# Eight transformer layers on one core: from layer after layer to one order for the whole program

## The chip, the cores and the metric

The kernel runs on one core of a Trainium2 chip. The metric is the device time of one launch in microseconds; the kernel before was run three times, and one more execution was profiled.

## The reference

A sequence model of four blocks, each an attention-like layer and a feed-forward layer with a layer norm in front and a residual around it: eight layers on x of 8 batch elements x 512 tokens x 128 channels, all float32.

```python
x = x + _L0_attn_ref(_layernorm(x), ...)   # 16 heads of 8; scores set to 0 where the key's 32-block is later than the query's
x = x + _L0_ffn_ref(_layernorm(x), ...)    # gated SiLU of width 352, inputs and weights rounded to FP4 in blocks of 16
x = x + _L1_attn_ref(_layernorm(x), ...)   # causal, with ALiBi; q, k, v weights plus low-rank terms
x = x + _L1_ffn_ref(_layernorm(x), ...)    # ternary weights: 128 -> 512 (gated) -> 512 -> 512 -> 128, two GELUs
x = x + _L2_attn_ref(_layernorm(x), ...)   # full attention, no output projection
x = x + _L2_ffn_ref(_layernorm(x), ...)    # channel mix with the previous token
x = x + _L3_attn_ref(_layernorm(x), ...)   # convolution of 4, scan with decay 0.95, gate, its own layer norm
x = x + _L3_ffn_ref(_layernorm(x), ...)    # 2 branches x 8 experts of rank 64, running sums, a softmax router
```

In the expert layer `Q = x W_Q^T` and `K = x W_K^T`, the second branch uses `Q W_inv^T` and `K W_inv^T`, each expert multiplies a projection of Q with the running sum of a projection of K, and the sum over experts goes through `W_O`. All of these maps are linear up to that product, and a running sum along the tokens commutes with a map of the channels.

## The kernel before

All of x stays in SBUF as eight tiles `xs[b]` of 128 x 4 x 128 (four groups of 128 tokens). `tile_transformer` runs the layers one after another, each a function with pools of its own: `layer_block_attention`, `layer_fp4_ffn`, `layer_lora_attention` (causal), `layer_ternary_ffn`, `layer_full_attention`, `layer_channel_mix`, `layer_ssm`, `layer_experts`. Weight packs are fetched by `opened(...)` between the layers, on the SP queue, into memory that an earlier layer has given up.

The three attentions share `attention`. For each batch element three generators stand in it. `prep` normalises (statistics on DVE, the normalisation on POOL, L196), transposes, projects q and k, splits each into a rounded part and a rest (POOL, L213 and L214), writes both to DRAM and reads them back spread over 128 partitions (SP; `spread_q`, `spread_k`, `arrive`). `shift` multiplies all scores once (L287, pairs of 64-row products side by side; causal adds masks, L297) and takes their maxima (DVE, L302), which go back as two rows of q. `values` multiplies the scores again (L412, masks L420), takes the exp on ACT (L425), and sums with the values in four column groups of PE (`av`, L348), then transposes, divides and projects. q and k are two buffers deep (`NB = 2`). The order of these generators is written by hand: each is given a due time from a pace per layer and from a few durations, and the most overdue goes next.

```python
unit = {"block": 40.0, "causal": 36.0, "full": 46.0}[kind]
...
live.append([(b - 1) * unit, 1.0, prep(b)])
live.append([b * unit, (unit - 1) / (shift_us + 1), shift(b)])
live.append([(b + 1) * unit + 8.0, unit / values_us, values(b)])
```

The other layers are loops `for b in range(B): one(b)` whose order the tile framework's own scheduler sets, with pools two deep. In `layer_fp4_ffn` the helper `fp4` finds a scale per block of 16, multiplies by its inverse on POOL (L677), rounds by comparisons that are added up on DVE (L680 to L686), scales back on POOL (L687) and puts the sign back; it is called on the normalised input (512 columns) and on the hidden units (1408 columns). In `layer_ternary_ffn` PE does 16 products of 512 columns for each of two hidden layers (L778), ACT the GELU out of PSUM (L779). In `layer_experts` q, k and their inverses are four products (L931), each of eight expert groups has two products (L986, L987), a product that spreads the router's weights (L989) and one that sums (L996); the output product is L1003. PSUM holds two double banks ("wide"), three single ones and one for sums.

Of the kernel before, what the change touches and what calls it, by code (L numbers as in the profile page):

```python
# [20 lines left out]
P = 128  # L21
# [6 lines left out]
CROW = 8  # L28
I_FFN = 352
NBLK_I = I_FFN // 16  # L30


@with_exitstack
def tile_transformer(ctx: ExitStack, tc: tile.TileContext, d: dict, out: bass.AP, layout: dict):
    nc = tc.nc
    wpool = ctx.enter_context(tc.tile_pool(name="weights", bufs=1))
    small = ctx.enter_context(tc.tile_pool(name="small", bufs=4))
    act = ctx.enter_context(tc.tile_pool(name="act", bufs=2))
    psum = ctx.enter_context(tc.tile_pool(name="psum", bufs=1, space=PSUM))
    dram = ctx.enter_context(tc.tile_pool(name="dram", bufs=2, space=bass.MemoryType.DRAM))  # L40

    def const(shape, name, dtype=F32):
        return wpool.tile(shape, dtype, name=name, tag=name)

    def wide(name):
        return psum.tile([P, 2, 512], F32, tag="wide", name=name, bufs=2)

    def bank(name, tag="ring"):
        return psum.tile([P, 512], F32, tag=tag, name=name, bufs=3 if tag == "ring" else 1)
# [5 lines left out]
    packs = {}  # L55

    def load_pack(name, engine, pool=None):
        rows, n = d[name].shape
        t = (pool or wpool).tile([rows, n], F32, name=f"pack_{name}", tag=f"pack_{name}")
        engine.dma_start(out=t, in_=d[name])  # L60
        packs[name] = t

    nc.sync.dma_start(out=xs[0], in_=x_in[0])
    first = ctx.enter_context(ExitStack())
    load_pack("l0a", nc.scalar, first.enter_context(tc.tile_pool(name="first", bufs=1)))
    nc.sync.dma_start(out=xs[1], in_=x_in[1])
    n_rows = d["rows"].shape[0]
    rows_t = const([P, n_rows], "rows")
    nc.gpsimd.dma_start(out=rows_t, in_=d["rows"].partition_broadcast(P))
    for b in range(2, B):  # L70
        nc.sync.dma_start(out=xs[b], in_=x_in[b])

    def w(pack, field):
        off, n = layout[pack][field]
        return packs[pack][:, off : off + n]

    def row(field):
        off, n = layout["rows"][field]
        return rows_t[:, off : off + n]


    ident = const([P, P], "ident")
    make_identity(nc, ident)
    ident_bf = const([P, P], "ident_bf", BF16)
    make_identity(nc, ident_bf)
    tri_ij = const([P, P], "tri_ij", BF16)
    make_causal_mask(nc, tri_ij, -BIG)
    tri_ji = const([P, P], "tri_ji", BF16)
    nc.gpsimd.memset(tri_ji, 0.0)
    nc.gpsimd.affine_select(  # L90
        out=tri_ji, in_=tri_ji, compare_op=ALU.is_ge, fill=-BIG, base=0,
        pattern=[[1, P]], channel_multiplier=-1,
    )
    ones = const([P, T], "ones")
    nc.gpsimd.memset(ones, 1.0)
    nhalf = const([P, NT], "nhalf")
    nc.gpsimd.memset(nhalf, -0.5)


    def moments(src, name, eps=1e-5):  # L100
# [3 lines left out]
        for t in range(NT):  # L104
            nc.vector.bn_stats(st[:, t, :], src[:, t, :])
            nc.vector.bn_aggr(mv[:, t, :], st[:, t, :])
        ve = small.tile([P, NT], F32, tag="ve", name=f"ve_{name}")
        nc.gpsimd.tensor_scalar(ve, mv[:, :, 1], eps, None, ALU.add)
        rstd = small.tile([P, NT], F32, tag="rstd", name=f"rstd_{name}")
        nc.gpsimd.tensor_tensor(rstd, ve, nhalf, ALU.pow)  # L110
        return mv, rstd

    def normalized(src, name, eps=1e-5):

        mv, rstd = moments(src, name, eps)
        xn = act.tile([P, NT, D], F32, tag="xn", name=f"xn_{name}")
        for t in range(NT):
            nc.vector.tensor_scalar(
                xn[:, t, :], src[:, t, :], mv[:, t, 0:1], rstd[:, t : t + 1], ALU.subtract, ALU.mult
            )  # L120
        return xn

    def transposed(src, name, dst=None, tag="xT", engine=None):

        ps = bank(f"ps_{name}")
        for t in range(NT):
# [348 lines left out]
    def raw(ap):  # L475

        return ap.bitcast(F32)
# [707 lines left out]
```

## Time and profile before

| | us |
|---|---|
| median of 3 runs | 3034.66 (3018.61 to 3059.03) |
| profiled execution, its time | 3029.08 |
| its span, first to last instruction | 3027.1 |
| PE busy | 2300.0 (76%) |
| DVE busy | 1410.9 (47%) |
| ACT busy | 1070.1 (35%) |
| POOL busy | 446.0 (15%) |
| mean granted clock of PE | 0.812 |

By stage, from the first and last instruction of each layer: start to 62 us, block attention to 515, fp4 to 944 (its work ends near 880, the rest is the next layer's start), causal attention to 1461, ternary to 1787, full attention to 2272, channel mix to 2355, ssm to 2623, experts to the end. "Busy" is the union of the time of an engine's instructions in a stretch; matmuls overlap each other, so a busy PE may still have room. The granted clock is the share of PE's full clock that the chip allowed. A share of busy time over the whole span mixes stages with different limits: it is read stage by stage.

### The profile page before, as it was taken

Reading aid. Unit: us, or ns where it says so; the run is one execution under the profiler, and the core shown is the slowest. Engines: PE = TensorE matmul, PEld = TensorE weight load, DVE = VectorE, ACT = ScalarE, POOL = GpSimd, SP = SyncE. Lnnn points to the kernel's source line nnn. Section 1 sums busy time; section 2 is a strip of 40 time slices with the busy share of each in tenths; the row PEclk is TensorE's granted clock in tenths of the full one; section 3 lists DMA queues with packets and bytes.
Section 4 is the critical chain, followed back from the end, with each engine's and each line's share of the span. In section 5 each row is a group of like instructions: output and inputs, shape, how many; then the busy total and the mean of one; then the engine's idle time right before and its main releaser. Section 6 shows DMA issues by size and latency. Waiting matters only on the chain.

```text
span 3027.1 us, 30970 instructions
## 1 busy us (share of the span) xinstructions
PE 2300.0 (76%) x12145; PEld 1086.0 (36%) x12145; DVE 1410.9 (47%) x2294; ACT 1070.1 (35%) x2190; POOL 446.0 (15%) x506
## 2 busy tenths in 40 slices
PE   2899897322224999999999968999884555699998
PEld 0444443221122454444444433333323222234343
DVE  2656552677643444552111128877824444433223
ACT  0466554111110454454322213777671111122122
POOL 4211200121221111110000021111102212200000
PEclk9899996666665687786799986999997666688888
DMA  6332210000014222220000023232200000000000
GB/s 134 102 97 82 89 31 16 0 0 0 0 69 101 58 86 72 58 71 2 1 0 1 0 68 99 72 97 60 71 2 0 27 0 0 0 4 7 4 7 7
DMA packets 61553, 120.69 MB, mean 40 GB/s; under 512 B 6360, under 2 KB 14840, under 8 KB 61024
## 3 DMA queue, kind: packets, MB, share of 16 engines
q1 hardware_dynamic: 60512, 117.11, 13.7%
q8 instruction: 96, 1.57, 0.2%
q10 hardware_dynamic: 496, 1.19, 0.1%
q0 software_dynamic: 400, 0.41, 0.1%
q14 instruction: 49, 0.40, 0.0%
HBM read 60.89 MB, written 52.43 MB: 37 GB/s over the span
## 4 chain that ended last, share of the span: by engine, by line
PE 68%; DVE 14%; ACT 7%; POOL 5%; issue 3%; SPq 2%; DMA 2%; DVEq 0%; ACTq 0%; POOLq 0%
PE psh_t L778 7%; PE s_causal L412 4%; PE av_block L348 4%; PE av_causal L348 4%; PE av_full L348 4%; PE s_full L412 3%; PE s_block L412 3%; PE s_causal L287 3%; PE acc_m L996 3%; PE s_full L287 2%; PE psb_m L989 2%; PE psvw_m L986 2%; PE ps_t L768 2%; PE psvw_m L987 2%; ACT e_full L425 2%
## 5 line engine op out<-in xcount | busy, mean ns | idle before, releaser
L302 DVE TENSOR_REDUCE mx_full<-s_full 128x2 f32<-128x1024 f32 x256 | 301.5, 1219 | 85.6 <-PE s_full L287 85.4
L302 DVE TENSOR_REDUCE mx_causal<-s_causal 128x2 f32<-128x768 f32 (+3 forms) x176 | 196.6, 1127 | 252.9 <-PE s_causal L297 252.0
L425 ACT ACTIVATE e_full<-s_full 128x512 f32<-128x512 f32 x512 | 270.2, 601 | 106.7 <-PE s_full L412 104.9
L302 DVE TENSOR_REDUCE mx_block<-s_block 128x2 f32<-128x768 f32 (+3 forms) x176 | 194.5, 1124 | 178.8 <-PE s_block L287 173.3
L425 ACT ACTIVATE e_causal<-s_causal 128x256 f32<-128x256 f32 (+3 forms) x512 | 196.1, 435 | 222.5 <-PE s_causal L420 222.3
L425 ACT ACTIVATE e_block<-s_block 128x256 f32<-128x256 f32 (+3 forms) x512 | 191.0, 443 | 97.8 <-PE s_block L412 93.7
L736 PE MATMUL pshT_f<-ident,acc_hf 128*128 128x128 f32 (+1 forms) x96 | 22.5, 423 | 227.4 <-DVE acc_hf L688 227.4
L412 PE MATMUL s_full<-q_full,k_full 64*128 64x512 f32 x512 | 159.0, 445 | 26.4 <-ACT e_full L425 25.6
L412 PE MATMUL s_block<-q_block,k_block 64*128 64x256 f32 (+3 forms) x512 | 147.0, 410 | 26.9 <-ACT e_block L425 16.9
L287 PE MATMUL s_full<-k_full,q_full 62*128 62x512 f32 x512 | 129.3, 501 | 44.6 <-DVE mx_full L302 26.6
L287 PE MATMUL s_causal<-k_causal,q_causal 62*128 62x512 f32 (+3 forms) x512 | 110.4, 482 | 68.1 <-DMA k_causal<-spread_kcausal 61.7
L412 PE MATMUL s_causal<-q_causal,k_causal 64*128 64x256 f32 (+3 forms) x512 | 153.3, 508 | 3.8 <-ACT e_causal L425 3.2
L348 PE MATMUL av_full<-e_full,va_full 128*32 128x512 f32 x1024 | 137.5, 610 | 0.0
L287 PE MATMUL s_block<-k_block,q_block 62*128 62x512 f32 (+3 forms) x512 | 89.4, 379 | 57.4 <-DMA k_block<-spread_kblock 42.1
L348 PE MATMUL av_causal<-e_causal,va_causal 128*32 128x512 f32 (+3 forms) x1024 | 126.6, 577 | 0.0
L412 PEld LDWEIGHTS s_block<-q_block,k_block 64*128 64x128 f32 x512 | 76.0, 197 | 124.9 <-ACT e_block L425 78.4
L140 DVE TENSOR_TENSOR x<-ps_t,x 128x512 f32<-128x512 f32 x8 | 5.5, 691 | 239.5 <-PE ps_t L784 239.5
L778 PE MATMUL psh_t<-g_t,pack_l1f 128*128 128x512 f32 x256 | 111.2, 592 | 0.0
L778 PE MATMUL psh_t<-h_t,pack_l1f 128*128 128x512 f32 x256 | 111.2, 592 | 0.0
L287 PEld LDWEIGHTS s_full<-k_full,q_full 62*128 62x128 f32 x512 | 53.2, 202 | 158.9 <-DVE mx_full L302 70.9
L412 PEld LDWEIGHTS s_full<-q_full,k_full 64*128 64x128 f32 x512 | 67.6, 187 | 108.0 <-ACT e_full L425 96.1
L412 PEld LDWEIGHTS s_causal<-q_causal,k_causal 64*128 64x128 f32 x512 | 72.1, 227 | 95.2 <-ACT e_causal L425 56.9
(410 smaller groups left out, 3773.3 us busy)
## 6 DMA issues: line engine op xcount, KB each, us to landing
spread_qblock<-cq_block SPq DMA_DIRECT2D x8, 1024.0 KB
spread_kblock<-ck_block SPq DMA_DIRECT2D x16, 512.0 KB
q_block<-spread_qblock SPq DMA_DIRECT2D x32, 256.0 KB
k_block<-spread_kblock SPq DMA_DIRECT2D x32, 256.0 KB
spread_qcausal<-cq_causal SPq DMA_DIRECT2D x8, 1024.0 KB
spread_kcausal<-ck_causal SPq DMA_DIRECT2D x16, 512.0 KB
q_causal<-spread_qcausal SPq DMA_DIRECT2D x32, 256.0 KB
k_causal<-spread_kcausal SPq DMA_DIRECT2D x32, 256.0 KB
```

The lines of the kernel that those rows point to most:

```text
L287: nc.tensor.matmul(s[:, j, gi, :], lhsT=q[rows, p0 + gi, ti * P : (ti + 1) * P], rhs=k[rows, p0 + gi, 0:n], start=gi == 0, stop=not tri an ...
L302: nc.vector.tensor_reduce(mx[:, ti, :, p0 : p0 + ng], s, AX.X, ALU.max)
L348: nc.tensor.matmul(av[r : r + 32, i0:T], lhsT=lhsT, rhs=rhs, start=first, stop=last, skip_group_check=True)
L412: nc.tensor.matmul(ps[:, i0:T], lhsT=k[rows, p, tj * P : (tj + 1) * P], rhs=q[rows, p, i0:T], start=True, stop=not tri, skip_group_check=tri,)
L425: nc.scalar.activation(et[:, 2 * u + j, i0:T], ps[:, i0:T], AF.Exp)
L736: nc.tensor.transpose(ps[0:n, t * P : (t + 1) * P], hq[:, t, o : o + n], ident)
L768: nc.tensor.matmul(ps[:, m, :], lhsT=wt[:, c * P : (c + 1) * P], rhs=xT, start=True, stop=True)
L778: nc.tensor.matmul(ps, lhsT=wt[:, a : a + P], rhs=h[:, ic, :], start=ic == 0, stop=ic == 3)
L986: nc.tensor.matmul(ps[:, 0, :], lhsT=w("l3f", wn)[:, cs], rhs=ks[br], start=True, stop=True)
L987: nc.tensor.matmul(ps[:, 1, :], lhsT=w("l3f", vn)[:, cs], rhs=qs[br], start=True, stop=True)
L989: nc.tensor.matmul(psb, lhsT=sel[:, br * 512 + c * P : br * 512 + (c + 1) * P], rhs=rw, start=True, stop=True)
L996: nc.tensor.matmul(acc, lhsT=w("l3f", un)[:, cs], rhs=pr, start=False, stop=br == 1 and c == 3)
```

## The change

The scheduler, all pools and the order of work are replaced; the arithmetic of the attentions is kept.

- An object `Plan` keeps a time for each engine and for the DMA and, for each tile, when it was last written and read. Every instruction goes through `Engine.call`, which adds its cost by a formula. The layers are generators ("streams") that yield what they need next: an engine, tiles, banks, slots. `Plan.run` takes, among those that could start soonest (within 0.15 us), the one with the lowest rank. The whole program is emitted in this one order, on all engines.
- Streams depend on streams of the same batch element: fp4 of element b on its block attention, causal attention of b on its fp4, and so on. The attentions run as 24 elements without a break between the layers; ranks put attention (0 to 4) ahead of fp4 (20), ternary (30) and the last three layers (40 and up).
- Memory: 36 slots of 128 x 512, two exp tiles, PSUM as four pairs of banks that give single banks or pairs; taken and given back by every stream. Weights are fetched into slots by streams of their own, on SP.
- Attention: q and k of a half of the heads are tiles of their own, so that a half can arrive earlier; two exp tiles, filled in turn (before, two or three); normalisation on POOL in block and full attention, on DVE in causal and for the first element of each layer.
- SiLU and sigmoid are written with tanh, which shares a table with exp; DVE does `(t + 1) * p` and the product. GELU takes its scale from a DVE instruction that takes the product out of PSUM. Fp4 treats the hidden units in three pieces (512, 512 and 384 columns), normalises on POOL.
- Experts: the projections by W_Q, W_K, W_inv are multiplied into the router's and the experts' weights once, W_O into the output maps and biases; the router's weights are spread with rounded (high and low) operands; the sum is formed with tokens on partitions, so that no output product is left. In ssm the two small products are merged into one matrix, and the first part of the convolution goes to ACT.

```diff
+class Plan:
+    def cost(self, key, op, out, ins, kw, args):
+        ...
+        if key == PE:
+            ...
+            if dt == F32R:
+                return 0.043 + 0.25e-3 * n
+            ...
+            return 0.02 + 1.67e-3 * n
+        if key == ACT:
+            return 0.19 + 0.82e-3 * n
+        ...
+    def run(self):
+            ...
+                first = min(r[0] for r in ready)
+                best = min((r for r in ready if r[0] <= first + 0.15), key=lambda r: (r[1], r[0], r[2]))[3]
...
+    slots = plan.pools["slot"] = Pieces(plan, [const([P, T], f"s{i}") for i in range(N_SLOTS)])
+    banks = plan.pools["bank"] = Banks(
+        plan, [psum.tile([P, 2, 512], F32, tag=f"pair{i}", name=f"pair{i}_") for i in range(4)]
+    )
+    ets = plan.pools["et"] = Pieces(plan, [const([P, 4, T], f"et{i}") for i in range(2)])
...
-                nc.scalar.activation(sg, ps[:, 0, :], AF.Silu, scale=s1[:, c : c + 1])
-                nc.vector.scalar_tensor_tensor(h[:, c, :], ps[:, 1, :], s2[:, c : c + 1], sg, ALU.mult, ALU.mult)
+            act.activation(a, p1, AF.Tanh, scale=hs[:, c : c + 1])
+            yield need(DVE, a)
+            dve.scalar_tensor_tensor(a, a, 1.0, p1, ALU.add, ALU.mult)
+            banks.give(p1)
+            dve.scalar_tensor_tensor(a, p2, hs[:, 4 + c : 5 + c], a, ALU.mult, ALU.mult)
...
-                        nc.scalar.activation(g[:, oc, :], ps, AF.Gelu, scale=s[:, oc : oc + 1])
+                dve.tensor_scalar(a, ps, s[:, oc : oc + 1], None, ALU.mult)
...
+            for a in g:
+                act.activation(a, a, AF.Gelu)
...
-                qT = product(w("l3f", "W_QT"), xT, "qT")
-                kT = product(w("l3f", "W_KT"), xT, "kT", scan=True)
-                qs = (qT, product(w("l3f", "W_invT"), qT, "qiT"))
-                ks = (kT, product(w("l3f", "W_invT"), kT, "kiT"))
+        dve.tensor_tensor_scan(kT, late["ones"], xT, 0.0, ALU.mult, ALU.add)
...
+                pe.matmul(ps, lhsT=late["vw"]["k", br][:, cs], rhs=kT, start=True, stop=True)
...
+                pe.matmul(ps, lhsT=sels[br][:, cs], rhs=rw, start=True, stop=True)
...
-    layer_block_attention()
-    first.close()
-    opened("lora", "l1a")
-    fp4_pack = opened("l0f")
-    layer_fp4_ffn()
-    ...
+    plan.add("causal", 8, causal_tables(), after=["half1_1"])
+    plan.add("fp4w", 9, fp4_weights(), after=["shift0"])
+    plan.add("ternw", 9, ternary_weights(), after=["att5", "causal"])
+    plan.add("fullw", 9, full_tables(), after=["att10"])
+    plan.add("latew", 9, late_weights(), after=["fullw", "tern4"])
+    plan.add("expertw", 9, expert_weights(), after=["latew", "tern7"])
+    ...
+    for e in range(3 * B):
+        ...
+        plan.add(f"prep{e}", 1, prep(e), after)
+        ...
+        plan.add(f"shift{e}", 4, shift(e), [f"prep{e}", "keys"] + ([f"shift{e - 1}"] if e else []))
+        plan.add(f"values{e}", 3, values(e), [f"shift{e}", f"pv{e}"] + ([f"values{e - 1}"] if e else []))
+    for b in range(B):
+        plan.add(f"quant{b}", 20 + b, fp4_ffn(b), [f"att{b}", "fp4w"] + ([f"quant{b - 1}"] if b else []))
+        plan.add(f"tern{b}", 30 + b, ternary_ffn(b), [f"att{B + b}", "ternw"] + ([f"tern{b - 2}"] if b > 1 else []))
+        plan.add(f"mix{b}", 40 + 3 * b, channel_mix(b), [f"att{2 * B + b}", "latew"])
+        plan.add(f"ssm{b}", 41 + 3 * b, ssm(b), [f"mix{b}"] + ([f"ssm{b - 1}"] if b else []))
+        plan.add(f"out{b}", 42 + 3 * b, experts(b), [f"ssm{b}", "expertw"] + ([f"out{b - 2}"] if b > 1 else []))
+    plan.run()
```

## The prediction

> **What bounds the kernel now.** First the forty slices of the span: PE is near full in most, but not in slices 7 to 12 and 29 to 34, and the granted clock is low there; it is low as well in slices 13 to 19, where PE is full.
>
> ```profile
> PE   2899897322224999999999968999884555699998
> PEclk9899996666665687786799986999997666688888
> ```
>
> Then the busy time by stage (cut where each layer's first and last instruction stand): block attention, fp4, causal attention, ternary, full attention, channel mix, ssm, experts. Columns are PE, PE load, DVE, ACT, POOL, clock, DMA share, GB/s.
>
> ```profile
> 62.00:515.00 453.00, 404.02 (x2988) 197.42 (x2988) 240.32 (x362) 239.01 (x604) 73.66 (x89) 0.92 0.24 69
> 515.00:944.00 429.00, 106.24 (x483) 79.29 (x483) 257.46 (x393) 55.12 (x91) 88.72 (x61) 0.63 0.08 20
> 944.00:1461.00 517.00, 502.37 (x4077) 243.83 (x4078) 237.01 (x340) 228.67 (x573) 64.61 (x82) 0.71 0.21 61
> 1461.00:1787.00 326.00, 317.98 (x945) 156.90 (x946) 39.71 (x89) 92.22 (x122) 6.91 (x10) 0.99 0.01 3
> 1787.00:2272.00 485.00, 409.52 (x2272) 157.36 (x2271) 342.22 (x417) 299.00 (x569) 88.05 (x103) 0.92 0.24 71
> 2272.00:2355.00 83.00, 41.63 (x176) 27.61 (x176) 39.37 (x89) 15.65 (x26) 23.64 (x29) 0.77 0.00 0
> 2355.00:2623.00 268.00, 137.25 (x284) 62.46 (x284) 114.85 (x306) 38.92 (x51) 60.45 (x73) 0.61 0.02 8
> 2623.00:3027.00 404.00, 374.75 (x912) 158.75 (x912) 128.64 (x285) 98.25 (x152) 10.25 (x16) 0.86 0.02 6
> ```
>
> Three kinds of stage: PE-bound at a full clock (ternary), PE-bound at a low clock (causal, 517 us at 0.71), and stages that no engine fills (fp4, mix, ssm: 780 us with PE busy 285). In the last kind one batch element's chain is followed almost alone, as the waits say: PE waits 227 us for fp4's DVE work, and twice a layer's start waits for the round trip through DRAM.
>
> ```profile
> PE pshT_f L736 <- DVE acc_hf L688: 227.4, 8, 28.9
> ...
> PE s_causal L287 <- DMA k_causal<-spread_kcausal: 61.7, 2, 60.9
> ...
> PE s_block L287 <- DMA k_block<-spread_kblock: 42.1, 4, 38.3
> ```
>
> **Prices.** From the groups, the longest chain pieces and PE's timeline:
>
> ```profile
> L302 DVE TENSOR_REDUCE mx_full<-s_full 128x2 f32<-128x1024 f32 x256 | 301.5, 1219 | 85.6 <-PE s_full L287 85.4
> L425 ACT ACTIVATE e_full<-s_full 128x512 f32<-128x512 f32 x512 | 270.2, 601 | 106.7 <-PE s_full L412 104.9
> ```
> ```profile
> 1476.65 27.47 PE psh_t L778 x64
> ```
> ```profile
> 1906.01 1.07 PE L348 MATMUL av_full<-e_full,va_full 128*32 128x512 f32 x8
> 1907.01 0.50 PE L287 MATMUL s_full<-k_full,q_full 62*128 62x512 f32 x2
> 1907.35 0.40 PE L412 MATMUL s_full<-q_full,k_full 64*128 64x512 f32 x2
> ```
>
> At full clock half a 512-column fp32 product takes 27.47/64 = 0.43 us, so a product 0.86; eight av halves take 1.00 (1906.01 to 1907.01); a pair of rounded score products 0.34. The same reading gives 0.22 for a 128-column product and 0.11 for a transpose. Maxima 1.22 us, exps 0.60; a POOL normalisation 0.79 (L196), a DVE one 0.34 (L118).
>
> **The change, engine by engine** (counts from the two programs' instruction lists). PE at full clock, before: 752 products of 512 columns 645 us, 580 of 128 columns 129, 713 transposes 79, scores 438, av 323, masks 72, rest 52: 1,738. After: 588 give 505, 911 give 202, 757 give 84, scores 451, av 323, masks 72, rest 26: 1,663. Merging the expert weights is most of the -75 (four projections and the output product per element go, the selector product is rounded); the merging itself costs some dozen products, once. PE busy times clock summed over the stages is about 1,930, since "busy" holds modelled overlap; I use 1,663 and keep 1,855 as its other end.
> DVE: 1,411 busy before; the after list at the same prices gives 1,561: +40 for 64 scaled ternary evacuations (0.62), +41 for the tanh form of silu (56 more of some 0.73), -41 for 120 normalisations gone to POOL, the rest from fp4 in smaller pieces and ssm and mix gates.
> ACT: 1,173 by durations, as before (1,184). But 1,203 of its instructions now wait for ACT's own semaphore, 210 before: exps that followed each other every 0.48 to 0.55 us follow at 0.60 or more, 60 to 180 us in all. POOL: 446 becomes 532. SP issues 627 transfers for 443, at 0.43 us 270 us in all: not a bound, though a late one holds the next.
>
> Where the work stands in the fixed order, us at full clock for PE:
>
> ```
>                               PE    DVE   ACT
> until element 0's exps        25     42     9
> block 0-7 + fp4 (25 of 35)   357    452   317
> causal 0-7 + fp4, ternary    453    396   316
> full 0-6 + ternary, mix, ssm 514    671   377
> full 7 + ssm, all experts    315    (both) 155
> ```
>
> So 780 us of stages that no engine filled are put beside attention; the experts are not, they all stand behind the last element's exps.
>
> **The sum.** Start: before, the first exp is at 103 us. Fewer loads stand ahead now; I take 95 (bounds 70 and 105). Block: DVE leads with 452. Fp4's POOL products collide with DVE: L686 runs 0.68 us alone and up to 2.96 beside one.
>
> ```profile
> L686 DVE SCALAR_TENSOR_TENSOR acc_f<-mag_f,acc_f x24: 671/679/2958, 522.6 to 835.3; 128x512 f32<-128x512 f32 x24
> ```
>
> About 50 such POOL products of 1.05 us here, two thirds of them met: +35. DVE full to 94% of the stage (its best filled engine, ternary's PE, had 98%): 520. The other end is 452.
> Causal: PE leads with 453. The clock decides: before, the same attention ran at 0.50 for 58 us while PE had no gap.
>
> ```profile
> 1183.00:1255.00 72.00, 71.21 (x728) 37.59 (x728) 39.33 (x48) 39.61 (x102) 11.93 (x14) 1.00 0.32 98
> 1255.00:1313.00 58.00, 58.00 (x382) 25.54 (x381) 28.13 (x70) 22.51 (x56) 11.27 (x16) 0.50 0.16 46
> ```
>
> Elements 8 to 12 (246) at causal's own 0.71: 347. Elements 13 to 15 (206) with dense ternary products, at 0.90 between 0.71 and 0.99: 229. With some waits 590; at full clock throughout 453.
> [...]
> Full: 514 at 0.95 is 541, near the 0.92 of this attention before; ACT (377 and 30 of own waits) and DVE (some 430) are 75 to 80% full beside it, so waits both ways: 575.
> Tail: 315 at the experts' 0.86 is 366; with the last element's chain 385.
> 95 + 520 + 590 + 575 + 385 = 2,165. The profiled run was 3,029.08 with a span of 3,027.1, and the median of three is 3,034.66: two us outside the span and a fifth of a per cent. I forecast **2,170**.
> [...]
>
> **What covers what.** Fp4 costs nothing on PE only while DVE has room in block attention: DVE was 240 of 453 there, and is asked for 452. If the cover fails the block part grows one for one. A POOL normalisation is 2.3 times DVE's, four per element: it delays the fill-in work's start, not attention's, as POOL has 75% free. A transfer late on SP holds the q, k and max rows queued behind it; next late is the max reduction, then the exps of the next element.
>
> **Rivals.**
> *Near-perfect packing* (15%): each part ends with its leading engine and the clock holds: 70 + 452 + 470 + 514 + 330 = 1,836, say 1,850. For it: ternary ran at 98%. Against: that stage has one leading engine, and causal's clock fell with no idle at all.
> *Poor packing* (20%): the order's account has no low clock; where PE runs at half, the order on DVE and ACT, made for full clock, makes them wait, and the eight PSUM banks, now shared by all layers, hold the score pairs. Before, the hand-made order paced elements at 40, 36 and 46 us (`unit`), and they came every 51, 58 and 51: 1.1 to 1.6 times. By 1.2 on the four parts at their full-clock leads (452 + 453 + 514 + 315 = 1,734, giving 2,081), the first five causal elements at 0.50 (+246) and the start (95): 2,420.
> *The transfers become the bound* (4%, slower): q and k of every element go out to DRAM and back, SP takes its transfers in order, and weight loads that wait for a free slot now stand among them. The round trip, met with nothing to hide it, cost 38.3 us at the start. Exposed in full at all 24 elements that is 919 us: 3,084. It decides from about 36 us exposed per element, where the total passes 3,034 by itself. Against: the buffers are two deep as before, where steady elements showed waits of this kind of 18 us in all of full attention.
> *The overlap isn't there*: excluded by the order itself for fp4, ternary, mix and most of ssm; true of the experts, and in the sum.
>
> **How the numbers follow.** My forecast's own band, 1,950 to 2,350, has 60%; near-perfect 15, poor 20, transfers 4, other trouble 1. The range takes the poor case and most of the good one in: 1,900 to 2,500. A measurement here tells about 2% from no change, so faster means under 2,974: all of the first three, 0.94; slower 0.05; between them 0.01.
>
> **What would show it.** Right: a span with PE busy over 85%, DVE over 65%, no stretch of 400 us with PE a quarter busy; first exp before 105 us; element periods near 65 us in block, 74 in causal, 82 in full; a clock under 0.85 in the causal elements; a tail of 350 to 400 us with expert work alone. Wrong: PE waits on DMA for q or k of more than 100 us in all; block elements well over 70 us, which would say that DVE with POOL is worse than priced; or causal elements at 57 us, which would say that fill-in work holds the clock up.

## The result, and the profile after

The changed kernel takes 3371.34 us (3355.21 to 3388.36, four runs) where the kernel before, on the same chip, takes 3046.85: a ratio of 1.110, 95% interval 1.098 to 1.122. It is slower by a tenth; I had forecast 2,170. The profiled execution took 3366.31 us with a span of 3364.6 and a mean clock of 0.765 (0.812 before).

The page's busy line and its slices of PE:

```profile
PE 2504.0 (74%) x12626; PEld 1155.2 (34%) x12626; DVE 1526.1 (45%) x2627; ACT 1054.7 (31%) x2197; POOL 552.5 (16%) x653
...
PE   4776778778788888888877787777777776665555
```

No stretch is nearly empty any more, as slices 7 to 12 were before, but none is full either: not one slice of PE has a 9, where the page before had twenty. The engines' sums came out near the prices (DVE 1,526 for 1,561, POOL 552 for 532; PE's busy time times its clock, summed over the stages below, is 1,911, where I had 1,855 as the upper end). The time was lost between instructions, and by a lower clock.

The stages, cut as in my sum: until element 0's exps, from there to the first causal exp, to the first exp of full attention, to the first exp of the last element, to the end. Columns: length, then busy time of PE, PE load, DVE, ACT, POOL, then clock, DMA share, GB/s.

```profile
0.00:106.00 106.00, 52.66 (x234) 27.80 (x234) 59.26 (x84) 8.72 (x13) 39.59 (x52) 0.85 0.58 143
106.00:843.00 737.00, 557.75 (x3471) 278.36 (x3469) 429.51 (x818) 274.81 (x673) 149.95 (x175) 0.71 0.18 52
843.00:1698.00 855.00, 716.42 (x4548) 341.79 (x4548) 385.11 (x635) 281.05 (x656) 78.45 (x93) 0.74 0.15 43
1698.00:2636.00 938.00, 722.57 (x2773) 276.80 (x2772) 391.11 (x555) 340.88 (x614) 114.13 (x138) 0.81 0.11 31
2636.00:3365.00 729.00, 454.58 (x1603) 230.49 (x1603) 261.10 (x539) 149.25 (x245) 170.39 (x196) 0.78 0.01 3
```

Predicted lengths were 95, 520, 590, 575 and 385; measured are 106, 737, 855, 938 and 729. From one element's first exp to the next one's there are 90, 103 and 134 us in block, causal and full attention. In the kernel before it was 51, 58 and 52, without other layers beside them.

The waits show no transfer in the way of PE: it waits for k twice, 3.9 us in all (the second line here), and its weight loads wait 1.2 us for q and k. PE waits a little everywhere, and the largest single share is for ACT's exps (the first line is one of four PSUM pairs: total, times, longest; the four come to 273 of the 850 us that PE waits in all). ACT loads no table from 15 to 1332 us, where fp4's tanh runs among the exps (one at 400.41 us, between two of them); 44 loads of 1.28 us follow.

```profile
PE pair__104 L55 <- ACT et L55: 85.5, 87, 4.5
...
PE pair__104 L55 <- DMA k<-mk: 3.9, 2, 3.0
```

**Exps and maxima take turns.** The windows of causal element 11: first while its exps run, then the 25 us after them. In the first answer only instructions on the tile of maxima are counted (PE, PE load, DVE), in the second those on the exps' tile (PE, PE load, ACT).

```profile
1136.00:1203.00 67.00, 0.00 (x0) 0.00 (x0) 0.00 (x0) 0.77 0.16 51
1203.00:1228.00 25.00, 0.00 (x0) 0.00 (x0) 18.59 (x18) 0.81 0.18 43
```
```profile
1136.00:1203.00 67.00, 11.74 (x112) 2.25 (x112) 23.30 (x63) 0.77 0.16 51
1203.00:1228.00 25.00, 1.06 (x16) 0.31 (x16) 0.30 (x2) 0.81 0.18 43
```

In 67 us of exps not one maximum of the next element runs, then 18 of its 22 follow in 25 us in which ACT is busy for 2. In the kernel before both shared one window (maxima, then exps, of causal elements):

```profile
1111.00:1171.00 60.00, 1.02 (x4) 0.38 (x4) 24.68 (x22) 0.73 0.25 70
```
```profile
1111.00:1171.00 60.00, 15.84 (x128) 2.86 (x128) 24.53 (x64) 0.73 0.25 70
```

The hand-made order handed out both by time (`unit`). The new one has `values` at rank 3 and `shift` at rank 4, and whoever is first by rank among those that can begin gets the turn. But taking turns is only a part of it: the 67 us themselves hold 23 us of exps, where before 60 us held the exps and the maxima.

**The tail is a chain.** `ssm{b}` waits for `ssm{b-1}`, so seven of the eight follow each other after the attentions, every 87 us, with one element's experts beside them. The chain of waits inside one element's experts (start, us, engine and tile; the longest pieces of it):

```profile
3002.05 0.70 DVE s L55
3002.84 0.70 DVE s L55
3003.59 1.16 PE pair__107 L55 x8
3004.75 0.86 PE pair__104 L55 x2
3005.61 0.87 PE pair__107 L55 x2
3006.57 0.70 DVE s L55
3007.32 2.02 PE pair__107 L55 x10
3009.34 0.87 PE pair__106 L55 x2
```

PE and DVE take turns here too: two of the eight chunks take 8.25 us (3002.05 to 3010.30, where the next piece of this kind starts), 5.78 of them PE, 2.10 DVE. Before, an element took 33 us in ssm and 50 in the experts; 87 for both "overlapped" is no gain over 83 in sequence.

**What the account itself says.** The account can be summed up by its own arithmetic: it ends at 2,769 us, at a full clock, with PE busy for 1,760 of them (64%). On its longest chain stand 583 us of exps and some 520 of maxima, which a good order would put beside each other, and some 2,550 handoffs at 0.12 us, 306 us. So 600 us of my error were written in the order before any chip ran it.

### The profile page after: what moved, and what is told of

It reads as the page before. It is cut to its first block, busy times and chain, and to the rows that moved or that the text cites. A ratio compares the mean times of both kernels' runs of the same rounds, so it can differ in the third digit from the quotient of the medians.

```text
span 3364.6 us, 33894 instructions
## 1 busy us (share of the span) xinstructions
PE 2504.0 (74%) x12626; PEld 1155.2 (34%) x12626; DVE 1526.1 (45%) x2627; ACT 1054.7 (31%) x2197; POOL 552.5 (16%) x653
## 5 line engine op out<-in xcount | busy, mean ns | idle before, releaser
L55 PE MATMUL pair__104<-s,s 128*128 128x128 f32 (+4 forms) x988 | 323.9, 494 | 86.5 <-DVE s L55 43.4
L55 PE MATMUL pair__107<-s,s 128*128 128x128 f32 (+4 forms) x898 | 282.9, 478 | 62.0 <-DVE s L55 30.1
L55 PE MATMUL pair__105<-s,s 128*128 128x128 f32 (+5 forms) x826 | 257.5, 461 | 51.8 <-DVE s L55 24.2
L55 PE MATMUL pair__106<-s,s 128*128 128x128 f32 (+5 forms) x796 | 261.2, 513 | 40.6 <-DVE s L55 20.2
L55 DVE TENSOR_REDUCE mx_a<-pair__105 128x2 f32<-128x1024 f32 (+3 forms) x187 | 216.1, 1156 | 76.7 <-PE pair__105 L55 76.3
L55 ACT ACTIVATE et<-pair__105 128x512 f32<-128x512 f32 (+3 forms) x397 | 188.8, 496 | 180.9 <-PE pair__105 L55 61.6
L55 ACT ACTIVATE et<-pair__106 128x512 f32<-128x512 f32 (+3 forms) x357 | 168.8, 487 | 231.9 <-PE pair__105 L55 75.6
L55 ACT ACTIVATE et<-pair__104 128x512 f32<-128x512 f32 (+3 forms) x380 | 182.5, 498 | 176.5 <-PE pair__107 L55 61.9
L55 ACT ACTIVATE et<-pair__107 128x512 f32<-128x512 f32 (+3 forms) x402 | 190.8, 496 | 139.1 <-PE pair__107 L55 45.7
L55 DVE TENSOR_REDUCE mx_a<-pair__107 128x2 f32<-128x1024 f32 (+3 forms) x156 | 180.7, 1158 | 99.2 <-PE pair__107 L55 85.0
L55 PEld LDWEIGHTS pair__104<-s,s 128*128 128x128 f32 (+2 forms) x988 | 155.0, 220 | 185.7 <-issue 62.5
L55 PE MATMUL pair__106<-et,va 128*32 128x512 f32 (+3 forms) x1408 | 199.6, 646 | 21.1 <-ACT et L55 14.0
L55 PE MATMUL pair__105<-q,k 64*128 64x512 f32 (+3 forms) x397 | 170.5, 505 | 54.0 <-ACT et L55 43.9
L55 PEld LDWEIGHTS pair__107<-s,s 128*128 128x128 f32 (+1 forms) x898 | 143.5, 226 | 159.8 <-issue 55.7
L55 PE MATMUL pair__107<-q,k 64*128 64x512 f32 (+3 forms) x402 | 168.2, 502 | 39.0 <-ACT et L55 30.5
L55 DVE TENSOR_REDUCE mx_a<-pair__104 128x2 f32<-128x1024 f32 (+3 forms) x136 | 158.0, 1162 | 85.3 <-PE pair__104 L55 78.7
L55 PE MATMUL pair__104<-q,k 64*128 64x512 f32 (+3 forms) x380 | 162.2, 498 | 41.2 <-ACT et L55 37.5
L55 DVE SCALAR_TENSOR_TENSOR s<-s,s 128x512 f32<-128x512 f32 (+5 forms) x261 | 174.3, 672 | 31.3 <-POOL s L55 26.4
L55 PE MATMUL pair__106<-q,k 64*128 64x512 f32 (+3 forms) x357 | 161.5, 508 | 28.7 <-ACT et L55 22.4
L55 PEld LDWEIGHTS pair__105<-s,s 128*128 128x128 f32 (+2 forms) x826 | 129.0, 220 | 122.8 <-issue 40.4
L55 PEld LDWEIGHTS pair__106<-s,s 128*128 128x128 f32 (+2 forms) x796 | 122.6, 219 | 124.1 <-issue 56.4
L55 DVE TENSOR_REDUCE mx_a<-pair__106 128x2 f32<-128x1024 f32 (+3 forms) x129 | 149.4, 1158 | 27.5 <-PE pair__106 L55 21.7
```

The costliest lines, as they stand in the source:

```text
L55: return emit(*args, **kw)
```

## The experiments

Theory A: the overlap works, but inside each layer the pipelining made by hand is gone; streams with one or two elements in flight and fixed ranks make chains on which engines take turns. Theory B: mixing layers costs, by the clock and the shared banks. Theory C: the account lacks the low clock (my poor-packing rival). D and E, on the clock, came later and stand in the expectations of e6 and e9. All times are medians; ratios are to the kernel before on the same chip.

| run | us | ratio, 95% interval |
|---|---|---|
| e1_serial | 3737 | 1.228 (1.222 to 1.233) |
| e2_ssm2 | 3218 | 1.056 (1.052 to 1.061) |
| e3_account_pe | 3287 | 1.080 (1.075 to 1.084) |
| e4_account_handoff | 3170 | 1.042 (1.037 to 1.047) |
| e5_serial_paced | 3645 | 1.202 (1.190 to 1.214) |
| e6_before_extra_product | 3068 | 1.011 (1.002 to 1.020) |
| e7_paced_alone | 3459 | 1.142 (1.133 to 1.151) |
| e8_all_chains | 2931 | 0.966 (0.959 to 0.974) |
| e9_after_extra_product | 3532 | 1.168 (1.156 to 1.180) |
| e10_serial_paced_extra | 3887 | 1.285 (1.272 to 1.297) |
| e11_all_chains_extra | 3127 | 1.032 (1.019 to 1.045) |
| e12_all_but_pacing | 2987 | 0.987 (0.978 to 0.997) |
| e13_before_merged | 2945 | 0.974 (0.965 to 0.983) |

Of the three below 1, only e8's interval lies wholly more than 2% below the kernel before.

### e1_serial: the overlap taken out

```diff
-            after.append(f"{before[kind]}{b}")
+            after += [f"{before[kind]}{i}" for i in range(B)]
...
-        plan.add(f"tern{b}", 30 + b, ternary_ffn(b), [f"att{B + b}", "ternw"] + ...
+        plan.add(f"tern{b}", 30 + b, ternary_ffn(b), [f"att{B + i}" for i in range(B)] + ["ternw"] + ...
```

The same is done for `quant`, `mix` and `ssm`; `mix` also waits for the one two elements before it.

> The changed kernel with its layers made to follow each other again: every stream of a layer waits for all eight elements of the layer before. Theory A (chains): the overlap works, but inside each layer the new order has lost the hand-made pipelining; a layer's streams hold one or two elements at a time and each step waits for the one before on another engine. Then the layers, taken apart, are each longer than in the kernel before: attention near 85 us per element in block and causal where it was 51 and 58, ssm near 87 where it was 33, and the whole about 3,900 us (3,750 to 4,050), so the overlap was worth some 500 us. Theory B (mixing costs): the mixed stream itself is what hurts, through the low granted clock and the shared PSUM banks; taken apart, the stages come back to their lengths before (453, 429, 517, 326, 485 and so on) and the whole to about 3,050 us (2,950 to 3,200), with ternary at a clock near 0.99.

3,737 us: the overlap is worth 366 us, less than the 500 I gave it, and B is out as the main cause: taken apart, the attention stages do not come back to their lengths before. The stages from the first exp on, to be laid beside those of the kernel before (block, fp4, causal, ternary, full, channel mix, then ssm with the experts):

```profile
104.00:704.00 600.00, 440.17 (x2795) 195.32 (x2793) 202.04 (x311) 236.46 (x605) 61.49 (x80) 0.73 0.16 48
704.00:1101.00 397.00, 132.74 (x704) 118.76 (x704) 296.52 (x665) 50.17 (x88) 106.51 (x112) 0.60 0.00 0
1101.00:1822.00 721.00, 602.98 (x4096) 282.87 (x4096) 230.74 (x320) 230.51 (x576) 41.45 (x52) 0.56 0.18 52
1822.00:2206.00 384.00, 330.20 (x936) 155.07 (x936) 119.35 (x234) 67.21 (x111) 12.96 (x23) 0.98 0.02 7
2206.00:2931.00 725.00, 522.02 (x2313) 180.16 (x2313) 322.65 (x372) 305.32 (x582) 72.07 (x85) 0.75 0.17 49
```

Block, causal and full attention are 189, 204 and 240 us longer than before (they end 704, 721 and 725 us after their start, where it was 515, 517 and 485), ternary is 58 longer, fp4 32 shorter. So 633 of the 704 us by which the serial form's span is longer lie inside the attention layers, whose products and exps are the old ones. Of an element's 22 or 32 maxima mostly 4 or 5 began during the exps before it (17, 16 and 26 in the kernel before).

### e2_ssm2: two elements of ssm in flight

```diff
-  ssm(b), [f"mix{b}"] + ([f"ssm{b - 1}"] if b else []))
+  ssm(b), [f"mix{b}"] + ([f"ssm{b - 2}"] if b > 1 else []))
```

> The changed kernel with one dependence loosened: an element's ssm may begin when the ssm two elements before it is done, instead of the one before it. Theory A: the tail behind the last exps (661 us) is seven ssm chains of 87 us, one after another, on engines that are half idle; with two in flight it falls by about 150 us, and the total to 3,220 us (3,170 to 3,280). Theory B and a tail bound by PE (PE has 50 to 60% busy there): within 30 us of the changed kernel, 3,340 to 3,400.

3,218 us, as A said: after the last exp 528 us instead of 666, an element every 65 us instead of 87, with the same work. One name in a list of dependences cost 153 us.

### e3_account_pe and e4_account_handoff: other numbers in the account

```diff
-            return 0.02 + 1.67e-3 * n
+            return 0.02 + 2.1e-3 * n
```
(e3; the prices of rounded products and 32-column sums rise alike)
```diff
-            end += 0.12
+            end += 0.2
```
(e4)

> The changed kernel with PE's costs in the account raised by a quarter, which is near what a mean clock of 0.77 makes of them; only the order changes. Theory C (my poor-packing rival as I wrote it: the order was made for a full clock and therefore makes engines wait): the order now fits and the time falls to 3,000 us or below. Theory A: the chains are the same whatever PE is thought to cost, so 3,300 to 3,450, no gain.

> The changed kernel with the account's time between an instruction's end and its result's use on another engine raised from 0.12 to 0.20 us; only the order changes. Theory A with handoffs as the mis-sized cost (adding 0.08 us to each of the 2,500 or so handoffs that stand on the longest chain of the account makes about 200 us): an order that leaves room for them gains 100 to 150 us, 3,220 to 3,270. If handoffs do not matter: 3,340 to 3,400. Theory C says nothing of it.

e3: 3,287 us. 84 us better than the changed kernel, a little more than A allowed, far from C's 3,000: the account's clock was not the main thing that made the order bad. e4: 3,170 us, 202 better, more than either said. I do not call the handoff mis-measured: the changed kernel's trace has 0.03 to 0.10 us (medians by pair of engines) between a producer's end and a waiting consumer's start. The larger number changes which stream goes first: the last exp ends at 2,580 us instead of 2,698, and 586 us are left after it instead of 666. Why this order is so much better stays open. The 84 us of e3 may be of the same kind, since every number in the account moves the order, and no run shows by how much it moves the time by chance.

### e5_serial_paced and e7_paced_alone: maxima beside exps again

```diff
+                    due = max(0, steps - 5) * 64 // (total - 4) if e else 0
+                    steps += 1
-                    yield need(PE, q, k, pair=1, when=lambda: (e, hb) in arrived)
+                    yield need(PE, q, k, pair=1, when=lambda: (e, hb) in arrived and (e == 0 or exps[e - 1] >= due))
...
-        plan.add(f"shift{e}", 4, shift(e), ...
+        plan.add(f"shift{e}", 2.5, shift(e), ...
```

`exps[e]` counts the exps issued. e7 also keeps PSUM pair 0 for the maxima.

> The kernel of e1_serial (layers one after another, 3,737 us) with the maxima of the next element ranked ahead of the exps of this one and handed out by their count: the first five at once, the rest spread evenly over the 64 exps. In e1_serial only 4 or 5 of an element's 22 or 32 maxima began while the exps of the element before ran (17, 16 and 26 in the kernel before), and the rest came after the last exp, with ACT idle; elements came every 82, 87 and 90 us. Theory A1 (exps and maxima take turns because of their ranks): most maxima now run beside exps, full's elements come every 70 us or less, and the whole falls by some 200 us to 3,530 (3,450 to 3,600). Rival A2 (an attention element is bound by PE at its low clock, whatever the ranks): within 50 us of 3,737.

> The changed kernel (3,371 us) with the maxima paced and ranked as in e5_serial_paced and one of the four PSUM pairs kept for them. Theory A (several chains pace the program in turn): block attention gains some 50 us, but in causal and full attention the maxima wait for fp4's and ternary's results, which are last in rank and two at a time, so the whole stays within 60 us of 3,371. Rival (the turn-taking of exps and maxima is the main loss in the overlapped order too, as it is in the serial one): 200 us or more off, 3,170 or below.

e5: 3,645 us, 92 off, between the two. The turn-taking is gone (16 of 22 and 26 of 32 maxima now begin during exps), and elements come every 68 and 81 us in block and full attention (77 and 85 in e1), not the 70 or less for full that A1 gave. Causal got slower, 83 to 89: there PE's clock went from 0.57 to 0.53. So turn-taking cost something in this form, but 92 us are a small part of the 633 that its attention layers had lost; what holds the rest is not shown (PE at its low clock, A2, fits causal attention alone). e7: 3,459 us, 88 slower than the changed kernel. Block elements come every 81 us (90 before the edit), causal ones every 133 (103). Mended alone, this chain makes things worse. The edit does two things at once, since the pair kept for the maxima is lost to all other streams; no run tells them apart.

### e8_all_chains and e12_all_but_pacing: the edits together

The edits of e2, e4 and e7 (with a lead of seven maxima instead of five), and these:

```diff
-                best = min((r for r in ready if r[0] <= first + 0.15), ...
+                best = min((r for r in ready if r[0] <= first + 0), ...
-        plan.add(f"quant{b}", 20 + b, ...
+        plan.add(f"quant{b}", 5, ...
-        plan.add(f"tern{b}", 30 + b, ...
+        plan.add(f"tern{b}", 5, ...
-        xT = yield from normal_transposed(xs[b], nm, pool, 9)
+        xT = yield from normal_transposed(xs[b], nm, pool, 6)
```

The last is in `channel_mix`; the parts of fp4 get rank 5 as well. e12 is e8 without the edit of e7.

> The changed kernel with all of it together: maxima paced with a PSUM pair of their own, two elements of ssm in flight, fp4 and ternary at rank 5 (between the maxima and the weights) instead of 20 to 37, handoffs of 0.20 us in the account, the stream that can begin first always taken (no window of 0.15 us), mix content with six spare slots instead of nine. Theory A: each removes a chain that the next would have hidden, so that they give more together than singly: 2,890 us (2,830 to 2,960), below both kernels, with PE over 80% busy and a tail after the last exps of 300 us or less where it was 661. If the overlapped order is bound by something else (clock, banks, PE itself): the two gains already measured (153 for ssm, 202 for handoffs) do not add up, and it stays above 3,047.

> The kernel of e8_all_chains (2,931 us) without the pacing of the maxima and without the PSUM pair kept for them; the rest as there. Alone, that edit made the changed kernel 88 us slower. Theory A (the chains hide one another, so that one edit has no price of its own): together with the others it is worth 60 us or more, so this run is at 3,030 (2,990 to 3,090). Rival (pacing is simply a loss in an overlapped order, and the others give all of the gain): 2,930 or below.

e8: 2,931 us, faster than both kernels. Its page:

```profile
PE 2300.8 (79%) x12626; PEld 1078.7 (37%) x12626; DVE 1535.1 (52%) x2627; ACT 1063.3 (36%) x2197; POOL 545.2 (19%) x653
```

PE is 79% busy, not the 80 I asked for. What is left after the last exp takes 275 us instead of 666: six of the eight ssm elements and four of the experts now begin before it ends, where there were two and one. The clock rose to 0.833, with PE busy for 79% of the span instead of 74%.

Attention is hardly quicker, 91, 104 and 122 us per element; the last exp ends at 2,652 (2,698 in the changed kernel). Yet the two things that seemed to hold it are gone: 13 to 19 of 22 maxima, and 16 to 27 of 32, now begin beside the exps of the element before, and each element of full attention starts 150 us or more after its ternary has ended, where it started at that end. The same three stretches do hold more of the other layers' work (PE's busy time times its clock is 417, 615 and 686 us, where it was 396, 530 and 585):

```profile
112.00:844.00 732.00, 548.73 (x3579) 281.69 (x3575) 469.36 (x917) 286.65 (x685) 163.62 (x191) 0.76 0.19 56
844.00:1710.00 866.00, 750.60 (x4730) 344.03 (x4730) 387.70 (x614) 300.55 (x679) 70.23 (x87) 0.82 0.14 42
1710.00:2656.00 946.00, 753.74 (x3379) 317.46 (x3380) 509.60 (x778) 413.86 (x739) 201.96 (x242) 0.91 0.10 31
```

So the run shows that the tail's work can stand beside attention. What makes an attention element of the mixed order take 90 us and more it leaves open.

e12: 2,987 us. Pacing, a loss of 88 alone, is worth 56 here (I said 60 or more, with 2,990 as the lower end); the rival is out. But it does not quicken attention here either: without it elements come every 85, 94 and 126 us, and the last exp ends at 2,522 us, 130 earlier than in e8. The gain lies in what is left then, e12 first, e8 second:

```profile
2523.00:2982.00 459.00, 349.21 (x1297) 190.99 (x1296) 218.17 (x434) 99.91 (x156) 110.50 (x131) 0.89 0.02 5
2656.00:2927.00 271.00, 202.11 (x741) 112.22 (x740) 117.84 (x246) 54.01 (x84) 69.84 (x81) 0.87 0.02 5
```

An edit of such an order has no price of its own.

### e6, e9, e10, e11: the clock

One more product, its result overwritten, ahead of every pair of score products (causal alone in e6; block and causal in the others, where it stays out of the account, so that the order is untouched):

```diff
+ nc.tensor.matmul(
+     pair[0][:, i0:T], lhsT=k[:, p, tj * P : (tj + 1) * P], rhs=q[:, p, i0:T],
+     start=True, stop=True, skip_group_check=True,
+ )
```

> The kernel before, with one extra rounded product (128 rows, up to 512 columns, its result overwritten) ahead of every pair of score products in causal attention, 32 per element: 256 of 0.07 to 0.17 us, some 30 us of PE at full clock. It asks what the low clock of causal attention (0.71 over 517 us, 0.50 for 58 us with PE never idle) hangs on. Theory D (it hangs on how little of the array the 64-row products and the 32-column sums use): the clock of the stage rises above 0.85 and the stage falls to 450 us or less, the whole to 2,980. Without that: clock within 0.04 of 0.71, stage some 40 us longer, the whole 3,070 to 3,110.

> The changed kernel, order untouched, with the extra 128-row product of e6_before_extra_product ahead of every pair of score products in block and causal attention (512 in all, some 60 us of PE at full clock). In that run the clock of the five middle causal elements rose from 0.80 to 0.94 and their length did not change (57 and 59 us). Theory E (the low clock, 0.71 and 0.72 over the 1,536 us of block and causal, is a good part of what the changed kernel loses): the clock rises above 0.80 in both and the time falls by 80 us or more, to 3,290 or below. Theory A alone (chains, on which PE's products are a small part): the clock may rise, the time stays within 3,340 to 3,440.

> The kernel of e5_serial_paced (3,645 us) with the same extra product. There block elements came every 61 us and causal ones every 84 us at a clock of 0.53, where the kernel before has 58 at 0.80, though the same products stand in both. Theory E: in this form the low clock itself is the bound (0.53 times 84 is 45 us of full-clock time, 0.80 times 57.5 is 46); with the clock above 0.80 causal elements come every 65 us or less and the whole falls by 120 us or more, to 3,520. Otherwise 3,650 to 3,720.

> The kernel of e8_all_chains (2,931 us) with the same extra product in block and causal attention. With the chains shortened PE is nearer to being the bound there (its clock is 0.75 in block and 0.81 in causal attention). Theory E: 2,800 to 2,890. If the extra products cost what they take and the clock gains nothing: 2,940 to 3,000.

In e6 the clock was higher. The windows from the first to the last causal exp, in the kernel before and in e6:

```profile
989.00:1456.00 467.00, 462.51 (x3836) 222.49 (x3838) 202.03 (x292) 223.10 (x565) 52.49 (x67) 0.74 0.19 56
```
```profile
984.00:1475.00 491.00, 486.27 (x4099) 248.76 (x4103) 202.31 (x292) 223.90 (x566) 52.27 (x67) 0.86 0.18 53
```

From 0.74 to 0.86, and nothing gained: the stage is 24 us longer. D got its clock and lost its time. How much of the rise is the product's is less sure, since each value is from one execution. In e13, below, causal attention has the same instructions as in the kernel before, and its window reads:

```profile
982.00:1427.00 445.00, 436.67 (x3842) 213.94 (x3844) 202.22 (x293) 222.73 (x566) 53.23 (x68) 0.81 0.20 59
```

So one and the same stage had 0.74 in one execution and 0.81 in another, and 467 and 445 us. Over whole runs e6 had 0.800 to 0.825 and the kernel before, on that chip, 0.792 to 0.812, which points the same way as the windows.

In the other three the clock did not rise (first exp to last, without and with the edit: e9 0.72 and 0.71 in block, 0.73 and 0.71 in causal; e10 0.80 and 0.70, 0.53 and 0.55; e11 0.75 and 0.71, 0.81 and 0.81; whole profiled executions 0.765 and 0.754, 0.727 and 0.709, 0.833 and 0.822), and the 512 products cost 161, 242 and 196 us: 0.31 to 0.47 us each, against some 0.12 by the account's price at full clock. All three are above both ranges, so A as I put it was wrong in a point: PE's products are not a small part of the chain. The clock alone does not make 0.31 out of 0.12 (at 0.71 it would be 0.17, at 0.55 0.22). That each product stands on a chain, between the bank that ACT frees and its next exp, is argued and not shown.

### e13_before_merged: the merged weights alone

The kernel before, with

```diff
-                qT = product(w("l3f", "W_QT"), xT, "qT")
-                kT = product(w("l3f", "W_KT"), xT, "kT", scan=True)
-                qs = (qT, product(w("l3f", "W_invT"), qT, "qiT"))
-                ks = (kT, product(w("l3f", "W_invT"), kT, "kiT"))
+                nc.vector.tensor_tensor_scan(kT, ones, xT, 0.0, ALU.mult, ALU.add)
...
-                        nc.tensor.matmul(psg, lhsT=w("l3f", "router_w1T"), rhs=qs[br], ...
+                        nc.tensor.matmul(psg, lhsT=router[:, br * P : (br + 1) * P], rhs=xT, ...
```

and the other products on merged tiles alike.

> The kernel before with one part of the change alone: the expert weights merged once ahead of the experts (projections and the inverse into the router and the four expert products, the output product into the up-projections and the biases); the selector product stays as it was. Per element four projections and an output product go (4.3 us of PE at full clock, 34 us over eight elements), the merging costs some 17 products once (9 us). If this part is worth what its PE time is: the experts stage, 404 us at a clock of 0.86, falls by 25 to 35 us, and the whole to 3,010 (2,990 to 3,030 against a before of 3,040). If the chain of projections at the head of each element was what the stage waited for: 60 us or more off, below 2,980. If the stage only waits elsewhere: no change, 3,030 to 3,050.

2,945 us, a ratio of 0.974: 78 us off for 25 us of PE work. Not all of it is this edit's: in the two profiled executions, 91 us apart, full attention ends 30 us earlier, in layers that the edit leaves as they were, and 61 us fall behind that. An element's experts took 40 us instead of 50 (start of its first GELU to that of the next). The windows from the first element's to the last one's, before and in e13:

```profile
2636.20:2985.60 349.40, 330.43 (x800) 139.94 (x799) 105.94 (x207) 85.94 (x133) 3.98 (x7) 0.86 0.02 6
2611.60:2893.30 281.70, 278.17 (x1059) 157.94 (x1060) 104.25 (x204) 70.17 (x107) 2.53 (x4) 0.91 0.02 6
```

PE's idle time fell from 19 us to 4, so the chain at the head of each element was worth 15 of these 68 us; the rest is PE's own time, fewer products at a higher clock. The total fell in the range that I had given to the chain, but the chain was the smaller part. This part of the change is a gain; that it gave nothing in the new order, where the tail's elements came every 87 us by the ssm chain, is argued, since no run takes it out there.

## Why the prediction was wrong

**The step that failed is the length of each part**: "Block: DVE leads with 452 ... DVE full to 94% of the stage", "Causal: PE leads with 453", "514 at 0.95", "315 at the experts' 0.86 is 366". I took a part to be as long as its leading engine's work, at a fill near that of ternary, the best-filled stage of a hand-made order. The work was sized well: DVE was busy 430 us in the block part, where I asked for 452. The fill was not. DVE's there was 430/737, 58%. PE's, as my work over length times granted clock, was 357/523 = 68% in block, 453/633 = 72% in causal, 514/760 = 68% in full, 315/569 = 55% in the tail.

That the order is at fault, and not the work, e8 shows: it runs the same number of instructions on every engine in 440 us less. In the tail, forecast at 385 us and measured at 729, one cause is shown too: "mix, ssm" stood among the work put beside full attention, and of the ssm's eight elements seven began behind the last element's first exp, at 2,643 us and later, in a chain of 87 us each. One dependence changed took 153 us off (e2), and with the order changed the tail after the last exp fell from 666 to 275 us (e8). In the three attention parts, 845 us longer than forecast, the low fill is measured and its cause is open: the turn-taking of exps and maxima can be seen, but its removal gained 92 us in the serial form (e5) and did not shorten attention in the mixed one (e8 against e12).

**The clock** was the smaller term. I had 0.90 for the last causal elements, 0.95 for full and 0.86 for the tail; measured are 0.74 over causal, 0.81 and 0.78. With my fills and waits and the measured start and clocks the sum is 106 + 520 + 626 + 669 + 423 = 2,344. So of the 1,196 us that were missing some 170 are clock by itself, 11 the start, and a thousand are fill. The two are not independent: e9's products, some 60 us at full clock by the account, cost 161.

**One wait that is not there:** I had ACT's exps, waiting for ACT's own semaphore, follow each other at 0.60 us or more, 60 to 180 us in all. In the trace after, exps of 512 columns without a gap start 0.48 to 0.49 us apart, as in the kernel before.

**Of the rivals**, poor packing named the right direction and the wrong reason: the account's clock (e3) gave 84 us, and its factor of 1.2 was far too small. Its other reason, PSUM banks shared by all layers, does not account for e1, where no other layer ran beside attention and it was still 633 us longer. The transfers are refuted by the waits. That the overlap isn't there is refuted by e1 as a whole, but I excluded it for "most of ssm", and there it was true. In the sum of near-perfect packing no run shows the 470 us of causal attention: that part took 855 us at a clock of 0.74, and 866 at 0.82 in e8. None of my cases was an order whose own chains are longer than the kernel before; the slower side had only the transfers, at 4%.

**Of the signs**, PE over 85%, DVE over 65% and element periods of 65, 74 and 82 us all failed (74%, 45%; 90, 103, 134), as did the tail of 350 to 400 us (729); the first exp missed its 105 us by half of one. The clock below 0.85 in causal attention came, and no stretch of 400 us had PE a quarter busy. Block elements well over 70 us came too, but they do not say what I wrote of them: DVE was not worse than priced, 430 us busy where I had 452.

**What set the pace in full attention** is not shown: each element's start there coincides with the end of its ternary (1628, 1800, 1924, 2104, 2199, 2384 and 2525 us), which stood at rank 30 and above and two at a time. In e8, where no element waited for its ternary any more, they came every 122 us instead of 134, with more work beside them; e8 changed ternary's rank together with other things.

The clock in these rows does not go by PE's busy share: causal attention had 0.74 before with PE 99% busy and 0.56 in e1 with 84%, but fp4 in e1 had 0.60 with PE 33% busy, and the same causal instructions had 0.81 in e13 with PE 98% busy.

## What to carry to other kernels

Overlapping layers adds up only if each layer's own pipeline survives (here elements came every 90 to 134 us instead of 51 to 58); before pricing a new order by the work of its engines, look for two streams that used to share a window and now have different ranks, and for every "after the one before" in its dependences (one of these cost 153 us here). If the order comes from an account in the kernel, sum that account first: here the chip took a fifth longer than its end, and its longest chain named things that took turns on the chip, though mending one of them alone cost 88 us. Judge edits of such an order together, since they do not add up, and try the parts that are not order (here the merged weights) alone.

## What the runs showed of the hardware that I had not expected

With extra products on all 128 rows a stream without gaps read a clock of 0.86, where it read 0.74 and 0.81 in two executions without them; in streams where PE had gaps (81 to 89% busy) they did not raise it, and block attention lost up to 0.10. What decides between them was not found. The same products of block attention ran at 0.93 in the kernel before (103 to 508 us, 51 us per element) and at 0.73 in e1 (77 us). So a clock read from a stage before is no constant to be carried into a new order, nor, with 0.74 and 0.81 for the same instructions, even into the next execution.
